# Layer 0's cross-attention: PSUM in four pairs of banks, and one instruction for two heads' banks

## The chip, the cores and the metric

The kernel runs on one NeuronCore of a Trainium2 chip. Its engines work side by side, each on its own queue of instructions: TensorE (PE; its weight loads are shown apart as PEld) multiplies matrices, VectorE (DVE) and ScalarE (ACT) work on elements, GpSimd (POOL) does the same and issues some of the DMAs, SyncE (SP) issues the others. TensorE writes its results to PSUM, a small memory that VectorE and ScalarE read. This kernel uses it as eight banks of 512 float32 columns by 128 partitions. An engine that needs the result, or the buffer, of another waits for a semaphore. The metric is device time in microseconds (us), the median of several runs.

## The reference

The reference is a two-layer decoder on 32 sequences of 100 tokens of width 256. Each layer has self-attention, cross-attention to a context, and a mixture of experts, all in float32. The change lies in the cross-attention of Layer 0, with 16 heads of 16 channels and a context of 361 positions of width 128:

```python
Q = (x @ Wq.T).reshape(B, xN, NUM_HEADS, HEAD_DIM)
KV = (z @ Wkv.T).reshape(B, zN, 2, NUM_HEADS, HEAD_DIM)
K = KV[:, :, 0]
V = KV[:, :, 1]
attn = jnp.einsum('bqhd,bkhd->bhqk', Q, K) * SCALE
attn = jax.nn.softmax(attn, axis=-1)
O = jnp.einsum('bhqk,bkhd->bqhd', attn, V).reshape(B, xN, DIM)
return O @ Wo.T
```

For each sequence and head this is a table of 100 queries by 361 positions, of which each row's maximum, exponentials and sum are taken.

## The kernel before

The function `l0_xattn` does this part. All eight banks of PSUM are one ring of single banks (`banks("l0x", t=8)`). Every producer on TensorE asks for a bank by `bank(...)`, and when the ring is empty its first weight load waits until the last reader of the bank that is handed out is done. Banks come back in the order in which their readers are planned to finish.

The main loop runs over 64 items M, two per sequence b: M = 2b + c, where c picks eight of the 16 heads. Those eight heads are done in two groups j of four. The four heads of a group lie in four blocks of 32 rows (`rows_of(r)`), so that their matmuls run side by side on TensorE. A head has 16 channels. The other 16 rows of its block carry a row of ones and the negated maximum, so that the second product below comes out with the maximum already subtracted.

The order of TensorE's queue is written out by hand (`manual_schedule`); that of the other engines is set by the framework's planner. For item M, TensorE gets:

- `maxima(M - 1)`: two transposes of the maxima (L543), which VectorE adds to the queries (L545). One bank.
- `scores(M, 0)`: queries by keys for four heads, into four banks. VectorE takes each bank's maximum over 361 positions, 100x1 from 100x361 (L535): one instruction for each head.
- `turned(M - 1, 0)`: the same product turned, positions by queries, in three pieces of 121 positions by 100 queries for each of the four heads, into four banks. ScalarE takes the exponential of each bank, 121x300 (L557): one instruction for each head. GpSimd adds up pieces for the sums (L561, L562).
- `values(M - 2)`: exponentials by values (L571) and by ones (L578), into one bank, which ScalarE copies (L583).
- `scores(M, 1)` and `turned(M - 1, 1)`: the other four heads, four banks each.
- the extras: `keys` for the next sequence (one bank; ScalarE makes two masked copies, L507), then either `out` (the output projection of a finished tile of 128 tokens, when c is 0; VectorE adds it to x, L261) or `queries` (when c is 1, in every other pair of items; ScalarE, L500), or neither, then `vals` for the next sequence (one bank; two or four copies by ScalarE, L520).
- at some items a piece of the next part's work: the turning of normed rows (L231), or the routing's logits (L1414).

So an item asks for 21 banks or a few more, out of eight. `keys` runs in 62 of the items, `out` or `queries` right behind it in 36. The helper `mm` (L156) issues the matmuls of most of these. In the profile `ps_t<-k,qT` at L156 is `scores`, `ps_t<-q,k` is `turned`, `ps_t<-cT,wB` is `keys`, `ps_t<-wB,zT` is `out`, `ps_t<-xnT,wB` is `queries` and `ps_t<-wB,cT` is `vals`. One matmul in the code shows up there as two.

The reciprocal of the sums (L588, in `divided`) is made to stand behind the last reduction of a group with j = 0, by an explicit dependency.

Of the kernel before, what the change touches and what calls it, by code (L numbers as in the profile page):

```python
# [9 lines left out]
F32 = mybir.dt.float32  # L10
I32 = mybir.dt.int32
U32 = mybir.dt.uint32
AF = mybir.ActivationFunctionType
ALU = mybir.AluOpType
AX = mybir.AxisListType

P = 128
NB = 32
T = 100
NT = NB * T  # L20
NF = NT // P
D = 256
NK = D // P
H = 16
L = 361
NKC = 3
KC0, KC = 121, 124
# [72 lines left out]
class Kernel:  # L100
# [26 lines left out]
        return self.tc.tile_pool(name=f"ps{name}", bufs=1, space=bass.MemoryType.PSUM)  # L127

    def bank(self, tag):
        if tag not in self.n_banks:  # L130
            tag = "t"
        return self.psum.tile([P, 512], F32, tag=tag, name=f"ps_{tag}", bufs=self.n_banks[tag])

    def bank_s(self):
        return self.bank("s")
# [91 lines left out]
    def norm_turn(self, f, n, xn, bank):  # L227
        pt = bank[:, : NK * n * P].rearrange("p (k c) -> p k c", k=NK)
        for k in range(NK):
            for j in range(n):  # L230
                self.nc.tensor.transpose(  # L231
                    pt[:, k, j * P : (j + 1) * P], xn[:, j, k * P : (k + 1) * P], self.ident,
                )
        self.evac(self.xnT[:, :, f * P : (f + n) * P], pt)
# [197 lines left out]
    def l0_xattn(self):  # L432
        nc, tc, a = self.nc, self.tc, self.a
        with ExitStack() as st:
            self.psum = st.enter_context(self.banks("l0x", t=8))
            w = self.wts.tile([P, 3584], F32, tag="wB", name="wB0")
            wq = w[:, :512].rearrange("p (k n) -> p k n", k=NK)
            wk, wv = w[:, 512:768], w[:, 768:1024]
# [40 lines left out]
            ks = [cp.tile([P, 2, 2, LP0], F32, tag=f"k{i}", name=f"k{i}") for i in range(3)]  # L479
            ms = [cp.tile([T, 2, P], F32, tag=f"m{i}", name=f"m{i}") for i in range(3)]  # L480
# [2 lines left out]
            for t in ks:  # L483
                nc.gpsimd.memset(t[:, :, :, L:], 0.0)
            later = deque()
            ctx, q, q2, e, es = {}, {}, {}, {}, {}
            self.z_begin(pool, 2)

            def load(b):
# [10 lines left out]
                    nc.scalar.activation(t[:, c, j, :], pm, AF.Copy, scale=quarter[:, j : j + 1])  # L500

            def keys(b, c):
                pm = self.bank_t()[:, :L]
                self.mm(pm, [(wk[:, c * P : (c + 1) * P], ctx[b][:, :L])])
                t = ks[b % 3]
                for j in range(2):
                    nc.scalar.activation(  # L507
                        t[:, c, j, :L], pm, AF.Identity, bias=one[:, j : j + 1], scale=own[:, j : j + 1]
                    )

            def vals(b, c0, n):
                pm = self.bank_t()[:KC0, : n * D].rearrange("p (c d) -> p c d", c=n)
                for i in range(n):
                    c = c0 + i
                    self.mm(pm[:, i, :], [(ctx[b][:, c * KC0 : (c + 1) * KC0], wv)])
                pv = pm.rearrange("p c (h j d) -> p c h j d", j=2, d=16)
                v = vs[b % 3][:, c0 : c0 + n].rearrange("p c (h j) e -> p c h j e", j=2)
                for j in range(2):
                    for i in range(n):
                        nc.scalar.copy(v[:, i, :, j, 16 * j : 16 * j + 16], pv[:, i, :, j, :])  # L520

            def rows_of(r):
                return slice(32 * r, 32 * r + 32)


            def scores(M, j):
                b, c = divmod(M, 2)
                cols = slice((b % 4) * T, (b % 4 + 1) * T)
                ps = [self.bank("r")[:T, :L] for _ in range(4)]
                for r in range(4):  # L530
                    self.mm(ps[r], [(q[b // 4][rows_of(r), c, j, cols], ks[b % 3][rows_of(r), c, j, :L])])
                m = ms[M % 3]
                for r in range(4):
                    o = 32 * r + 16 * (1 - j)
                    got = nc.vector.tensor_reduce(m[:, j, o : o + 1], ps[r], AX.X, ALU.max, negate=True)  # L535
                return got

            def maxima(M):
# [7 lines left out]

            def turned(M, j):
                b, c = divmod(M, 2)
                ps = [self.bank("r")[:KC0, : NKC * T] for _ in range(4)]
                for i in range(NKC):  # L550
                    for r in range(4):
                        self.mm(ps[r][:, i * T : (i + 1) * T], [(
                            ks[b % 3][rows_of(r), c, j, i * KC0 : (i + 1) * KC0], q2[M][rows_of(r), j, :]
                        )])
                t = e[M, j] = pool.tile([KC0, 4, NKC, T], F32, tag="e", name="e", bufs=5)
                for r in range(4):
                    nc.scalar.activation(t[:, r], ps[r].rearrange("p (c t) -> p c t", c=NKC), AF.Exp)  # L557

                n = L - 2 * KC0
                s = es[M, j] = pool.tile([KC0, 4, T], F32, tag="es", name="es", bufs=4)  # L560
                nc.gpsimd.tensor_tensor(s, t[:, :, 0, :], t[:, :, 1, :], ALU.add)  # L561
                nc.gpsimd.tensor_tensor(s[:n], s[:n], t[:n, :, 2, :], ALU.add)  # L562
# [48 lines left out]
            def extras(b):  # L611

                k0, k1, v0, v1, o, x = [None] * 6
                if b + 1 < NB:
                    k0, k1 = (lambda: keys(b + 1, 0)), (lambda: keys(b + 1, 1))
                    v0, v1 = (lambda: vals(b + 1, 0, 2)), (lambda: vals(b + 1, 2, 1))
                if b > 1 and tile_of(b - 2) is not None:
                    o = lambda: out(tile_of(b - 2))
                b0, i = b // 4 * 4, b % 4
                if i < 2 and b0 + 4 < NB:  # L620
                    x = lambda: queries(b0 + 4, i)
                return k0, v0, o, k1, v1, x
# [11 lines left out]
            with tc.manual_schedule(engines={mybir.EngineType.PE}):  # L634
# [4 lines left out]
                for c in range(2):  # L639
                    keys(0, c)  # L640
                vals(0, 0, 2)
                vals(0, 2, 1)
                last = 2 * NB
                for M in range(last + 2):
                    b, c = divmod(M, 2)
                    if c == 0:
                        if b + 2 < NB:
                            load(b + 2)
                        ex = extras(b)
                    if 0 < M <= last:  # L650
                        maxima(M - 1)
                    if M in norms:
                        f, *at = norms[M]
                        f(*at)
                    for j in range(2):

                        got = scores(M, j) if M < last else None
                        if j == 0 and M > 2:
                            divided(M - 3, zs, got)
                        if 0 < M <= last:  # L660
                            turned(M - 1, j)
                        if j == 0 and M > 1:
                            zs = values(M - 2)
                    if M == last + 1:
                        divided(M - 2, zs, None)
                    for i in (0, 2, 1):
                        if ex[3 * c + i]:
                            ex[3 * c + i]()
                    if M not in norms or len(later) > 3:
                        for _ in range(1 + (len(later) > 3)):  # L670
                            if later:
                                later.popleft()()
# [1422 lines left out]
```

## Time and profile before

| | |
|---|---|
| median of three runs | 2956.52 us (2954.38 to 2960.02) |
| the profiled execution | 2956.08 us, its span 2954.3 us |
| granted TensorE clock, mean | 0.984 |
| PE busy over the span | 97% |
| VectorE, ScalarE, GpSimd busy | 61%, 48%, 31% |
| the changed stage | 585 to 1065 us of the span |
| L535, reductions of a bank | 512 of 524 ns, 239.6 us busy |
| L557, exponentials of a bank | 512 of 426 ns, 173.9 us busy |

A row of groups gives line, engine, operation, what is written from what, shapes, the number of instructions, their busy time together and the mean length of one, and the idle time just before them with who ended it. A timeline merges instructions of a kind that follow each other: start, length from the first's start to the last's end, engine, line, operation, count. Instructions of one engine overlap: the four reductions of a group take 1.85 us together, less than four times one.

### The profile page before, as it was taken

How to read it: one execution, taken by the hardware profiler on the slowest of the kernel's cores; microseconds unless marked ns; L12 is line 12 of the kernel's file. 1: busy time of each engine (PE TensorE's matmuls, PEld its weight loads, DVE VectorE, ACT ScalarE, POOL GpSimd, SP SyncE). 2: the span in 40 equal slices, each digit the busy share in tenths (PEclk: the TensorE clock that was granted, in tenths of full speed). 3: DMA queues.
4: the chain of work that ended last, by engine and by line, in shares of the span. 5: the costliest groups of instructions: out<-in, count | busy, mean ns of one | idle time of the engine just before them, and what ended most of it. 6: DMA issues, size and time to landing. Idle time of an engine off the chain costs nothing. (4 is left out here: it accounts for less than half of the span.)

```text
span 2954.3 us, 66469 instructions
## 1 busy us (share of the span) xinstructions
PE 2851.3 (97%) x26012; PEld 2172.6 (74%) x26012; DVE 1787.6 (61%) x5120; ACT 1412.4 (48%) x4261; POOL 913.0 (31%) x1040
## 2 busy tenths in 40 slices
PE   8999999999999999999998999999999999999993
PEld 7777777677777766888886667777777777776672
DVE  6666665577777762222224878676676776776553
ACT  5555555467676641222223224565666565657320
POOL 3222221266666536100003621011302213123373
PEclk9999999999999989999999999999999999999996
DMA  9880000000000004564553100010000000000396
GB/s 319 269 290 1 1 1 1 12 15 16 16 16 16 10 29 147 191 223 181 194 215 112 49 4 10 6 38 25 26 10 13 10 9 16 12 11 5 97 227 189
DMA packets 127510, 224.11 MB, mean 76 GB/s; under 512 B 39470, under 2 KB 105446, under 8 KB 120401
## 3 DMA queue, kind: packets, MB, share of 16 engines
q1 hardware_dynamic: 97264, 125.64, 13.3%
q0 software_dynamic: 26640, 90.80, 9.3%
q8 instruction: 210, 3.44, 0.5%
q10 hardware_dynamic: 3280, 3.28, 0.3%
q14 instruction: 116, 0.94, 0.1%
HBM read 152.09 MB, written 112.56 MB: 90 GB/s over the span
## 5 line engine op out<-in xcount | busy, mean ns | idle before, releaser
L1691 POOL DMA_INDIRECT x_d<-xr,slot x200 | 195.4, 977 | 676.0 <-ACT eT L786 556.3
L156 PE MATMUL ps_t<-xnT,wA 128*128 128x200 f32 (+1 forms) x1608 | 330.9, 350 | 1.5 <-DMA wA<-in_wq 1.0
L156 PE MATMUL ps_t<-cT,q 128*128 128x361 f32 x832 | 317.3, 470 | 0.0
L786 ACT COPY eT<-ps_t 124x384 f32<-124x384 f32 (+1 forms) x416 | 193.6, 474 | 224.7 <-PE ps_t L785 224.5
L156 PEld LDWEIGHTS ps_t<-xnT,wA 128*128 128x128 f32 x1608 | 272.1, 191 | 32.4 <-issue 14.5
L776 ACT ACTIVATE wBx<-ps_t,m 128x361 f32<-128x361 f32 x416 | 235.8, 568 | 121.7 <-DVE m L773 117.7
L535 DVE TENSOR_REDUCE m<-ps_t 100x1 f32<-100x361 f32 x512 | 239.6, 524 | 48.3 <-PE ps_t L156 48.1
L156 PE MATMUL ps_t<-xT,w 128*128 128x256 f32 (+1 forms) x1276 | 260.2, 364 | 0.7 <-ACT xT L150 0.7
L773 DVE TENSOR_REDUCE m<-ps_t 128x1 f32<-128x361 f32 x416 | 218.3, 526 | 60.3 <-PE ps_t L156 58.3
L156 PEld LDWEIGHTS ps_t<-xT,w 128*128 128x128 f32 x1276 | 223.7, 190 | 36.2 <-issue 9.3
L785 PEld LDWEIGHTS ps_t<-ident,wBx 128*124 128x124 f32 x1248 | 156.1, 139 | 123.4 <-issue 68.2
L358 POOL TENSOR_TENSOR e<-e,rz 100x400 f32<-100x400 f32 x128 | 109.3, 854 | 406.3 <-DVE rz L357 396.8
L557 ACT ACTIVATE e<-ps_t 121x300 f32<-121x300 f32 x512 | 173.9, 426 | 119.0 <-PE ps_t L156 118.9
L785 PE MATMUL ps_t<-ident,wBx 128*124 128x128 f32 x1248 | 203.9, 275 | 5.3 <-DVE m L1627 2.1
L354 ACT ACTIVATE e<-s,m 100x100 f32<-100x100 f32 x512 | 186.1, 365 | 20.7 <-DVE m L348 20.0
L156 PE MATMUL ps_t<-wA,cT 128*124 128x512 f32 x384 | 195.5, 597 | 0.0
L778 DVE TENSOR_SCALAR wBx<-wBx,sums 128x361 f32<-128x361 f32 x416 | 172.9, 416 | 9.9
L1344 DVE TENSOR_TENSOR h<-ps_t,g 128x256 f32<-128x256 f32 (+1 forms) x145 | 58.2, 401 | 188.4 <-ACT g L1343 188.4
L156 PEld LDWEIGHTS ps_t<-q,k 32*121 32x121 f32 x3072 | 127.9, 181 | 36.0 <-issue 11.3
L797 PEld LDWEIGHTS ps_t<-eT,v 124*64 124x64 f32 x3072 | 133.1, 137 | 16.4 <-ACT wBx L776 5.6
L1343 ACT ACTIVATE g<-ps_t 128x256 f32<-128x256 f32 (+1 forms) x145 | 52.9, 365 | 190.9 <-PE ps_t L156 190.9
L1280 POOL DMA_INDIRECT w<-w_d,wid x29 | 29.5, 1017 | 371.0 <-PE ps_t L1371 337.4
(329 smaller groups left out, 5817.8 us busy)
## 6 DMA issues: line engine op xcount, KB each, us to landing
x_d<-fill SPq DMA_DIRECT2D x16, 1284.0 KB, 22.2
we<-in_wexp SPq DMA_DIRECT2D x32, 384.0 KB, 4.6
cT<-in_ctxT SPq DMA_DIRECT2D x64, 186.0 KB, 2.3
xe_d<-zero SPq DMA_DIRECT2D x8, 1024.0 KB, 16.3
xe<-x_d SPq DMA_DIRECT2D x24, 321.0 KB, 3.8
sum<-fill SPq DMA_DIRECT2D x10, 640.0 KB, 8.9
xe<-xe_d SPq DMA_DIRECT2D x24, 256.0 KB, 2.7
y_d<-y SPq DMA_DIRECT2D x24, 256.0 KB, 8.4
```

Source lines behind the costliest of these rows:

```text
L156: self.nc.tensor.matmul(out, lhsT=l, rhs=r, start=(i == 0), stop=(i == n - 1))
L354: nc.scalar.activation(t[:, i, :], s[:, i, :], AF.Exp, bias=m[:, i : i + 1], accum_out=rz[:, i : i + 1])
L358: nc.gpsimd.tensor_tensor(t[:, h, :], t[:, h, :], self.last(rz[:, h], T), ALU.mult)
L535: got = nc.vector.tensor_reduce(m[:, j, o : o + 1], ps[r], AX.X, ALU.max, negate=True)
L557: nc.scalar.activation(t[:, r], ps[r].rearrange("p (c t) -> p c t", c=NKC), AF.Exp)
L773: self.after = nc.vector.tensor_reduce(m, ps, AX.X, ALU.max, negate=True)
L776: nc.scalar.activation(t, ps, AF.Exp, bias=m, accum_out=z)
L778: nc.vector.tensor_scalar(t, t, z, None, ALU.mult)
L785: nc.tensor.transpose(pt[:, c, :], es[n % 5][:, c * KC : (c + 1) * KC], self.ident)
L786: self.after = nc.scalar.copy(eT[:, :, i * P : i * P + w], pt[:, :, :w])
L797: nc.tensor.matmul(pz[64 * j : 64 * j + 64, i, :], lhsT=v[:, c, h * 64 : (h + 1) * 64], rhs=eT[:, c, o : o + T], start=(c == 0), stop=(c = ...
L1691: got = nc.gpsimd.indirect_dma_start(out=self.x1_d[:, :], out_offset=bass.IndirectOffsetOnAxis(ap=slot[:, j, k : k + 1], axis=0), in_=xr[: ...
```

## The change

PSUM is given out in this stage as four pairs of neighbouring banks in place of eight single ones. A caller of `bank` gets the first bank of a pair of its own; the second then lies unused. `scores` and `turned` take two pairs each, with two heads in a pair, and each pair is read by one instruction: one maximum over both heads' banks (100x2 from 100x722), one exponential over both (121x600). `keys` takes a pair and leaves its second bank to the `vals` that follow it, so that the two share a pair.

```diff
     def bank(self, tag):
+        if not self.n_banks:
+            return self.pair()[:, 0, :]
...
+    def pair(self):
+        return self.psum.tile([P, 2, 512], F32, tag="t", name="ps_t", bufs=4)
...
-            self.psum = st.enter_context(self.banks("l0x", t=8))
+            self.psum = st.enter_context(self.banks("l0x"))
...
             def keys(b, c):
-                pm = self.bank_t()[:, :L]
+                both[c] = self.pair()
+                pm = both[c][:, 0, :L]
...
             def vals(b, c0, n):
-                pm = self.bank_t()[:KC0, : n * D].rearrange("p (c d) -> p c d", c=n)
+                pm = both[c0 // 2][:KC0, 1, : n * D].rearrange("p (c d) -> p c d", c=n)
...
-                ps = [self.bank("r")[:T, :L] for _ in range(4)]
+                ps = [self.pair()[:T, :, :L] for _ in range(2)]
                 for r in range(4):
-                    self.mm(ps[r], [(q[b // 4][rows_of(r), c, j, cols], ks[b % 3][rows_of(r), c, j, :L])])
-                m = ms[M % 3]
-                for r in range(4):
-                    o = 32 * r + 16 * (1 - j)
-                    got = nc.vector.tensor_reduce(m[:, j, o : o + 1], ps[r], AX.X, ALU.max, negate=True)
+                    self.mm(
+                        ps[r // 2][:, r % 2, :],
+                        [(q[b // 4][rows_of(r), c, j, cols], ks[b % 3][rows_of(r), c, j, :L])],
+                    )
+                m = ms[M % 3].rearrange("t j (h r e) -> t j h r e", h=2, r=2)
+                for h in range(2):
+                    got = nc.vector.tensor_reduce(
+                        m[:, j, h, :, 16 * (1 - j)], ps[h], AX.X, ALU.max, negate=True
+                    )
...
-                ps = [self.bank("r")[:KC0, : NKC * T] for _ in range(4)]
+                ps = [self.pair()[:KC0, :, : NKC * T] for _ in range(2)]
                 for i in range(NKC):
                     for r in range(4):
-                        self.mm(ps[r][:, i * T : (i + 1) * T], [(
+                        self.mm(ps[r // 2][:, r % 2, i * T : (i + 1) * T], [(
...
-                for r in range(4):
-                    nc.scalar.activation(t[:, r], ps[r].rearrange("p (c t) -> p c t", c=NKC), AF.Exp)
+                for h in range(2):
+                    two = t[:, 2 * h : 2 * h + 2].rearrange("p r c t -> p r (c t)")
+                    nc.scalar.activation(two, ps[h], AF.Exp)
```

More of the change, by code (lines that the diff above doesn't have):

```diff
@@ L485, in l0_xattn @@
             later = deque()
-            ctx, q, q2, e, es = {}, {}, {}, {}, {}
+            ctx, q, q2, e, es, both = {}, {}, {}, {}, {}, {}
             self.z_begin(pool, 2)
```

## The prediction

> **What bounds the kernel now.** I read the page's 40 slices first, then the busy table of this stage, then the timeline of two of its steps, then its waits, and last the rows that price the instructions. The change touches only Layer 0's cross-attention, which runs from 585 to 1065 us. The slices say that TensorE is full nearly all the time; VectorE and ScalarE are not.
>
> ```profile
> PE   8999999999999999999998999999999999999993
> DVE  6666665577777762222224878676676776776553
> ACT  5555555467676641222223224565666565657320
> ```
>
> In the stage alone, the columns being the stretch, its length, and the busy time of PE, weight loads, VectorE, ScalarE and GpSimd:
>
> ```profile
> 600.00:1060.00 460.00, 449.93 (x8533) 350.60 (x8523) 349.49 (x851) 310.81 (x898) 278.68 (x351) 1.00 0.05 14
> ```
>
> PE is busy for 98% of it at a granted clock of 1.00, VectorE for 76%, ScalarE for 68%. So the stage's length is that of PE's queue plus PE's waits, and work taken from VectorE or ScalarE is worth nothing by itself. What such an instruction does to the time is settled by when it gives its bank back to PE. The timeline (start, length, engine, line, what, how many; in brackets the idle time before and who ended it) shows that:
>
> ```profile
> 715.61 0.87 PE L156 MATMUL ps_t<-k,qT 32*100 32x361 f32 x8
> 716.49 1.85 DVE L535 TENSOR_REDUCE m<-ps_t 100x1 f32<-100x361 f32 x4 [0.63 <-PE ps_t L156]
> 717.08 0.30 PEld L156 LDWEIGHTS ps_t<-cT,wB 128*128 128x128 f32 x2 [0.16 <-DVE m L535]
> 717.08 0.88 PE L156 MATMUL ps_t<-cT,wB 128*128 128x361 f32 x2
> 717.11 1.36 ACT L557 ACTIVATE e<-ps_t 121x300 f32<-121x300 f32 x4 [0.99 <-PE ps_t L156]
> 717.52 0.89 PEld L156 LDWEIGHTS ps_t<-wB,zT 128*128 128x128 f32 x4
> 717.79 1.03 PE L156 MATMUL ps_t<-wB,zT 128*128 128x256 f32 x4
> 718.32 1.22 ACT L507 ACTIVATE k<-ps_t,one,own 128x361 f32<-128x361 f32 x2
> ...
> 720.67 1.42 DVE L535 TENSOR_REDUCE m<-ps_t 100x1 f32<-100x361 f32 x3
> 721.35 1.02 PEld L571 LDWEIGHTS ps_t<-e,v 121*32 121x32 f32 x48
> ```
>
> The four scores of a group end together (715.61 + 0.87 = 716.48), and VectorE reduces their banks one after another. The first reduction ends at 717.02; 0.05 later PE starts `keys` (cT,wB), in that very bank. `keys` already waits for the first bank to come back: eight banks are just enough. The waits of the stage agree (total us, times, longest):
>
> ```profile
> PEld ps_t L156 <- DVE m L535: 8.6, 51, 0.5
> PEld ps_t L571 <- DVE m L535: 8.0, 14, 1.4
> PE ps_t L571 <- DVE m L535: 5.6, 7, 1.2
> ```
>
> 51 of the 62 calls of `keys` (L156) wait for a maximum, and so do about 20 calls of `values` (L571).
>
> **The change, part by part.** *Fewer, longer reductions.* 512 become 256, each over two banks. Their length:
>
> ```profile
> L535 DVE TENSOR_REDUCE m<-ps_t 100x1 f32<-100x361 f32 x512 | 239.6, 524 | 48.3 <-PE ps_t L156 48.1
> L348 DVE TENSOR_REDUCE m<-s 100x8 f32<-100x800 f32 x64 | 63.0, 985 | 2.0
> L557 ACT ACTIVATE e<-ps_t 121x300 f32<-121x300 f32 x512 | 173.9, 426 | 119.0 <-PE ps_t L156 118.9
> ```
>
> 361 columns take 524 ns and 800 take 985, so a column costs 461/439 = 1.05 ns and 722 columns 524 + 361 x 1.05 = 903 ns. Bounds: 524 (the second bank free) and 967 (two of today's in a row, 524 + 443, since four take 1.85 us and so follow each other by 0.443). I take 903, by the 800-column row. A whole group then takes 0.903 + 0.82 = 1.72 us, not 1.85: 0.13 saved per group, 128 x 0.13 = 17 us of VectorE. Nothing on PE waits for the end of a group, so this is worth 0; it would count only if VectorE were the bound. *Exponentials:* the four take 1.36 us, one 0.426, so they already follow each other by 0.311. Two of 600 columns take 1.22 to 1.36 by the same reasoning. Worth 0: PE takes the first of those banks again 1.5 us after they begin (715.61 against 714.07 in the step shown).
>
> [...]
>
> *`keys` waits for two banks.* With four pairs, `keys` is the first taker after two pairs of scores and two of `turned`, and must wait for one of those. The earliest is the first score pair, 0.903 us after the reduction starts in place of 0.533: +0.36 where it waits today. I went through all 62 calls and took, for each, start of the first reduction + 0.90 + 0.05 less the start of its weight load, where positive: 56 are delayed, 20.3 us in all. Behind it in PE's queue stand `out` or `queries`, `vals`, the turning of the maxima and the next scores, so all of PE is late by it; ScalarE's copies of the keys, which wait for PE, begin later too. At 0.967 instead of 0.903 it is 24; at 0.524 it is 0.
>
> *`values` waits the same way.* At 720.67 the reductions start, at 721.35 `values` start; the pair is back at 720.67 + 0.95 = 721.62: +0.27. The same count over 64 calls: 35 late, 11.2 us.
>
> *`out` and `queries`.* One of them follows `keys` in 36 steps and takes the second score pair, back at 1.72 + 0.05 = 1.77 us after the reductions' start. `keys`, started at 0.95, frees PE after 0.71 (0.41 + 0.30 for its two passes) at 1.66; and a weight load that has waited is not hidden (+0.105, as the first pass of `keys` today: 0.41 against 0.30). 1.77 + 0.105 - 1.66 = 0.215, x 36 = 7.7 us. If the pair of the first exponentials is taken instead (back at 1.35), 0.
>
> *`vals` in the second bank of `keys`' pair.* It takes no new pair and waits for nothing new, provided that one bank's reader does not hold up the other bank's writer. But the pair comes back only after the last copy of the values (720.49 in the step shown, against the next scores at 719.78). The second half of the next `turned` is what takes it, at about 720.54 against 720.37; +0.17, which `values` wait for anyway: 0. If instead the second half of the scores took it, `values` would come 0.54 late in place of 0.27, at up to 27 steps: +7 to +15.
>
> *Table loads.* After the stage's 6 norm roots ScalarE reloads its table (1283 ns) and the exponentials come late; the next scores then wait for a pair, not a bank, one spacing of 0.31 longer: 6 x 0.3 = 1.8 us.
>
> Sum: 20.3 + 11.2 + 7.7 + 0 + 1.8 = 41 us. The profiled execution took 2956.08 (span 2954.3 and 1.8 around it), 0.4 below the median of 2956.52. 2956.1 + 41 = 2997.
>
> **The rivals.** *Absorbed (2976).* Only `keys` is late, and what follows finds its pair free in the time lost. For it: after a late `keys` the next waits start later too. Against: a reduction starts when PE ends the scores, so every gate moves along with PE. 20 us.
>
> *The value copies gate the scores (3012).* As above, 0.54 x 27 = 15 on top of 2997, if none of it falls together with `values`' own wait. For it: 0.77 us of copies (L520) end after the next scores begin. Against: `out` and `queries` give their pairs back sooner, and the planner hands out what is free first.
>
> *A pair is guarded as a whole (3045).* If `vals`' matmul had to wait until ScalarE has read the keys: 718.32 + 1.22 = 719.54 and 0.05, where without it PE would come to `vals` 0.58 later than today's 718.44, at 719.02. 0.57 there, and up to 1.1 where no `out` or `queries` stands between them; 0.77 as a middle, x 62 = 48 on top of 2997. No row of before has two banks in one tile, so it can't be excluded.
>
> *Faster (2941).* VectorE is the real clock: PE's waits for L535 in this stage are 8.6 + 8.0 + 5.6 = 22 us, mostly in steps where rows of a norm push the reductions back; if groups that end 0.13 earlier pull these in, up to 15 us go. It decides only where a two-bank reduction takes less than 0.53 us, so that the first pair returns as soon as the first bank does now; the 800-column row says 0.90.
>
> **How the numbers follow.** A measurement of this kernel tells about 0.2% (6 us) from no change. As summed (2985 to 3008): 0.50. Absorbed (2965 to 2985): 0.17. Value copies (3008 to 3030): 0.14. Pair as a whole (3030 to 3065): 0.09. Faster: 0.06. Same, by shares of all of these: 0.04. The range takes the first three, 2966 to 3030, and leaves out 0.2: the last three and a sliver of the second. Faster 0.06, same 0.04, slower 0.90.
>
> **What would show it.** The new profile should have 256 reductions of about 903 ns with a group of 1.72 us; PE's weight loads of `keys` should start 0.05 us after a *two-bank* reduction's end, with idle time near 0.5 us before them, where it is 0.16 now; `values` should wait in over 50 steps; the two score groups of one step should lie as far apart as now, but for that. VectorE and ScalarE should be busy for less time in a longer stage. I am wrong if the reductions take much under 0.9, if `vals` waits for L507, or if the stage (480 us now) grows by less than 25 or more than 60 us.

## The result and the profile after

The changed kernel takes 3051.84 us (3050.38 to 3052.94) against 2955.45 before: a ratio of 1.0326, interval 1.0314 to 1.0338, or 96 us slower. The forecast was 2997 (2966 to 3030): the direction was right, the size less than half. Measured again (after_again below), the two stood at 3053.91 and 2958.22, 1.0327 (1.0311 to 1.0343).

All of it is in the changed stage. From the first reduction's start to the last one's end it took 477.8 us before and takes 573.0 now, 95.2 more. The slices of the page after, eight in a row (the stage) at 0.8 where all were at 0.9:

```profile
PE   8999999888888889999999899999999999999993
DVE  6666656466556555222222687776766666776553
ACT  5555545455555543122212323565655666666320
```

The stage alone, before and after (stretch, length, busy time of PE, weight loads, VectorE, ScalarE and GpSimd, granted clock, DMA share and GB/s):

```profile
585.00:1065.00 480.00, 468.97 (x8748) 363.74 (x8744) 362.53 (x883) 325.16 (x938) 287.03 (x362) 0.99 0.05 14
585.00:1165.00 580.00, 497.65 (x8865) 362.23 (x8864) 348.66 (x639) 321.69 (x689) 289.91 (x364) 0.96 0.04 12
```

VectorE has 14 us less to do than in the stage before (17 was the prediction's figure) and ScalarE some 3 us less (the longer window holds a little other work); PE stands idle for 82 of the 580 us, where it was 11 of 480. What it waits for, in total us, times, longest; two rows of before, then three of after:

```profile
PE ps_t L156 <- DVE m L535: 0.9, 3, 0.4
PE ps_t L156 <- ACT k L507: 0.2, 1, 0.2
PE ps_t L161 <- ACT k L513: 38.6, 48, 1.6
PE ps_t L161 <- DVE m L543: 23.0, 60, 0.7
PE ps_t L582 <- DVE m L543: 18.4, 42, 1.2
```

L513 is ScalarE's copies of the keys (L507 before), and the one that waits is `vals`. The next line is nearly all `keys`, the last `values`; both are waits for a maximum. The timeline of one step after the change:

```profile
726.75 1.73 DVE L543 TENSOR_REDUCE m<-ps_t 100x2 f32<-100x722 f32 x2 [0.77 <-PE ps_t L161]
727.71 0.30 PEld L161 LDWEIGHTS ps_t<-cT,wB 128*128 128x128 f32 x2 [0.55 <-DVE m L543]
728.53 0.73 PEld L161 LDWEIGHTS ps_t<-wB,zT 128*128 128x128 f32 x4 [0.52 <-DVE m L543]
728.53 1.13 PE L161 MATMUL ps_t<-wB,zT 128*128 128x256 f32 x4
728.62 1.20 ACT L513 ACTIVATE k<-ps_t,one,own 128x361 f32<-128x361 f32 x2
729.87 1.12 PE L161 MATMUL ps_t<-wB,cT 128*121 128x256 f32 x4 [0.21 <-ACT k L513]
```

`keys` (cT,wB) start 0.96 us after the reductions do, 0.59 before. `out` (wB,zT) waits for the second pair of maxima: its matmuls come 0.82 us after those of `keys`, 0.71 before, and, their weights not loaded ahead, take 1.13, 1.03 before. And `vals` (wB,cT) starts at 729.87, 0.05 after the keys' copies end at 728.62 + 1.20 = 729.82. It writes the other bank of the pair that they read. Where no `out` or `queries` lies between, PE stands still for 1.29 us in place of the 0.21 here:

```profile
719.29 0.87 PE L161 MATMUL ps_t<-cT,wB 128*128 128x361 f32 x2 [0.39 <-DVE m L543]
720.21 1.20 ACT L513 ACTIVATE k<-ps_t,one,own 128x361 f32<-128x361 f32 x2
721.45 0.69 PE L161 MATMUL ps_t<-wB,cT 128*121 128x256 f32 x2 [1.29 <-ACT k L513]
```

The joined instructions came out as priced: a reduction takes 905 ns (priced at 903), and two exponentials together 1.23 us in the steps read (priced at 1.22 to 1.36):

```profile
L543 DVE TENSOR_REDUCE m<-ps_t 100x2 f32<-100x722 f32 x256 | 221.8, 905 | 78.2 <-PE ps_t L161 78.0
L568 ACT ACTIVATE e<-ps_t 121x600 f32<-121x600 f32 x256 | 157.7, 668 | 141.3 <-PE ps_t L161 141.3
```

### The profile page after: what moved, and what is told of

Read it like the earlier page. It is cut to its first block, busy times and chain, and to the rows that moved or that the text cites. A ratio compares the mean times of both kernels' runs of the same rounds, so it can differ in the third digit from the quotient of the medians.

```text
span 3051.2 us, 65927 instructions
## 1 busy us (share of the span) xinstructions
PE 2870.7 (94%) x26012; PEld 2163.6 (71%) x26012; DVE 1770.2 (58%) x4864; ACT 1408.5 (46%) x4005; POOL 914.4 (30%) x1040
## 5 line engine op out<-in xcount | busy, mean ns | idle before, releaser
L543 DVE TENSOR_REDUCE m<-ps_t 100x2 f32<-100x722 f32 x256 | 221.8, 905 | 78.2 <-PE ps_t L161 78.0
L784 DVE TENSOR_REDUCE m<-ps_t 128x1 f32<-128x361 f32 x416 | 218.3, 526 | 59.7 <-PE ps_t L161 57.8
L568 ACT ACTIVATE e<-ps_t 121x600 f32<-121x600 f32 x256 | 157.7, 668 | 141.3 <-PE ps_t L161 141.3
L161 PEld LDWEIGHTS ps_t<-q,k 32*121 32x121 f32 x3072 | 121.9, 185 | 28.3 <-DVE q L555 11.2
```

What stands on the lines that cost most here:

```text
L161: self.nc.tensor.matmul(out, lhsT=l, rhs=r, start=(i == 0), stop=(i == n - 1))
L543: got = nc.vector.tensor_reduce(m[:, j, h, :, 16 * (1 - j)], ps[h], AX.X, ALU.max, negate=True)
L568: nc.scalar.activation(two, ps[h], AF.Exp)
L784: self.after = nc.vector.tensor_reduce(m, ps, AX.X, ALU.max, negate=True)
```

## The experiments

Chips differ: the kernel before took 2987.62 us on the one that ran vals_free, vals_own_pair and the two kv kernels, and 2956.01 and 2958.22 on the two others. So times are compared as ratios to the kernel before on the same chip, and beside them as lengths of the stage (first reduction's start to last one's end in the profile).

### vals_free: the wait of vals taken away

```diff
 # keys: the two copies
+    tc.add_to_no_dep_group(f"keys{b}_{c}", got.ins)
 # vals: each matmul
+    tc.declare_no_dep(got.ins, group=f"keys{b}_{c0 // 2}", reason="the pair's other bank")
```

The framework then sets no wait between those copies and `vals`; all other waits stay.

> The changed kernel, except that the matmul of vals is told not to wait for the copies of the keys, which read the pair's other bank. Theory A (a pair is guarded as a whole, and that wait is the larger half of the loss): PE's idle time before vals for L513, 37 us after the change, goes, and with it some of the half-clock stretches in the stage: 2990 to 3015 us, near the forecast's 2997. Theory B (the ring of four pairs is short in itself; a wait taken away in one place comes back at the next taker): 3035 to 3052 us.

Measured: 3023.06 us against 2987.62, 1.0120 of before (1.0096 to 1.0144). Run again beside the changed kernel on one chip:

> The changed kernel once more, to stand beside vals_free on one chip: 1.031 to 1.034 of before.

> vals_free once more, beside the changed kernel and before. Theory A in its sizes (the guard of the whole pair costs 37 us of waiting and some 18 us of half clock; the later return of the pairs costs the other 40): 1.012 to 1.015 of before, 50 to 60 us under the changed kernel.

Measured: 3053.91 us (1.0327) and 2996.90 us (1.0129, 1.0114 to 1.0145). The stage takes 517.5 us, not 573.8. What PE waits for in vals_free_again:

```profile
PE ps_t L161 <- DVE m L547: 22.9, 60, 0.7
PE ps_t L586 <- DVE m L547: 18.0, 31, 1.2
```

The line of the keys' copies is gone, and the two waits for maxima stay as they were, 23 and 18 us. So nothing came back at the next taker, as theory B would have had it. 57 of the 96 us go with that one wait. The two banks have nothing to do with each other in the program; the wait comes only from the framework, which ordered accesses to this tile of two banks as if it were one.

### vals_own_pair: no sharing

```diff
-                pm = both[c0 // 2][:KC0, 1, : n * D].rearrange("p (c d) -> p c d", c=n)
+                pm = self.pair()[:KC0, 0, : n * D].rearrange("p (c d) -> p c d", c=n)
```

> The changed kernel, with a pair of its own for vals, so that the pair of the keys is not shared and its other bank lies unused. Theory A: the wait for the keys' copies goes, a wait for the third pair in order comes, which is back about 0.4 us before it is wanted: 2995 to 3020 us. Theory B: one more pair per item out of four, so slower than the changed kernel: 3055 to 3080 us.

Measured: 3029.45 us, 1.0147 (1.0124 to 1.0169), a stage of 520.3 us, 2.8 more than vals_free's. One more pair per item costs next to nothing. Where `vals` follow `keys` directly they start 0.81 us after them in the mean of 26 steps, 0.74 in vals_free_again; behind `out` or `queries` they lose nothing. Which pair they get, the trace does not show. Theory B is out: the ring is not short in that sense. Sharing a pair, meant to spare one, was the dear part.

### kv_pair_t6 and kv_single_t6: the same two banks as one tile and as two

Both start from the kernel before, with single instructions, and in both the first sequence's `vals` stand right behind each of its `keys`.

```diff
 # kv_pair_t6 (six single banks besides)
+                both[c] = self.psum.tile([P, 2, 512], F32, tag="kv", name="ps_kv", bufs=1)
+                pm = both[c][:, 0, :L]
...
+                pm = both[c0 // 2][:KC0, 1, : n * D].rearrange("p (c d) -> p c d", c=n)
 # kv_single_t6 (six single banks besides)
+                pm = self.bank("k")[:, :L]
...
+                pm = self.bank("v")[:KC0, : n * D].rearrange("p (c d) -> p c d", c=n)
```

> The kernel before, all instructions as they were, but with keys and vals in the two banks of one tile of their own and six single banks for the rest. To be compared with kv_single_t6, which uses the same banks as two tiles. Theory A: slower than kv_single_t6 by 62 waits of 0.5 to 0.9 us, 30 to 55 us. Theory B: the same within 6 us. Both are slower than before, since six banks do not hold two groups of four: 3010 to 3090 us.

> The kernel before with one single bank for keys, one for vals, and six for the rest. Theory A and B alike: slower than before, because the last two heads of turned must wait for reductions (0.5 to 1 us in each of 128 groups, less 8 us since keys no longer wait): 3000 to 3060 us.

Measured: 3244.84 us (1.0884, 1.0836 to 1.0932) and 3124.71 us (1.0457, 1.0430 to 1.0483), 120 us apart; stages of 727.0 and 623.4 us in the profiled executions. The sign is theory A's; the size, 104 us in the stage, is twice what it allowed. The waits of kv_pair_t6 hold only half of it; in kv_single_t6 the first line does not appear and the second reads 53.3:

```profile
PE ps_kv L156 <- ACT k L508: 57.8, 62, 1.5
PE ps_t L156 <- DVE m L536: 51.1, 120, 1.0
```

The other half is in PE's own speed. The two stages, kv_pair_t6 and then kv_single_t6:

```profile
590.00:1320.00 730.00, 620.17 (x8737) 450.87 (x8738) 358.92 (x878) 326.11 (x929) 287.71 (x360) 0.90 0.04 9
```

```profile
588.00:1212.00 624.00, 566.65 (x8732) 425.82 (x8728) 359.89 (x878) 323.63 (x930) 287.87 (x360) 0.96 0.04 11
```

The same matmuls take 54 us longer, at a mean granted clock of 0.90 in place of 0.96. By the trace's clock records PE ran at half its clock for 144.9 us of the one stage and 47.8 of the other; 97 us more at half the clock hold up to 48.5 us less work, an estimate from these two figures. 57.8 + 48.5 = 106 at most, against 103.6 measured. That the waits bring the half clock is not shown by this pair; the next run tests it.

### keep_busy: PE given something to do in the wait

The changed kernel, its wait of `vals` left as it is.

```diff
+                    tc.add_to_no_dep_group(f"keys{b}_{c}", got.ins)     # keys: the two copies
...
+                for _ in range(fill):            # vals: ahead of its own matmuls
+                    got = nc.tensor.matmul(
+                        pm[:, 0, :], lhsT=ctx[b][:, :KC0], rhs=wv, start=True, stop=True
+                    )
+                    tc.declare_no_dep(got.ins, group=f"keys{b}_{c0 // 2}", reason="the pair's other bank")
 # fill is 2 where no out or queries stands between keys and vals, else 0
```

> The changed kernel, and where vals follows keys directly, two extra matmuls (128x121 by 128x256) into the bank of vals are issued ahead of it; their result is overwritten. They do not wait for the keys' copies; vals still does. They fill about 0.86 us of a wait of 1.3 us in some 26 steps. If the half-clock stretches of the stage (41 us at half the clock, against 4 before) come from these waits and cost about 18 us, most of them go: 5 to 18 us faster than the changed kernel, 1.026 to 1.031 of before. If they come from elsewhere or cost nothing: the same as the changed kernel or slower, 1.032 to 1.040.

Measured: 1.0276 (1.0260 to 1.0292), 15 us less than the changed kernel by ratio. The stage takes 560.4 us in place of 573.0, with more matmuls in it. A step of keep_busy:

```profile
717.91 0.88 PE L161 MATMUL ps_t<-cT,wB 128*128 128x361 f32 x2 [0.38 <-DVE m L549]
718.62 1.03 PE L521 MATMUL ps_t<-wB,cT 128*121 128x256 f32 x4
718.83 1.19 ACT L513 ACTIVATE k<-ps_t,one,own 128x361 f32<-128x361 f32 x2
720.07 0.69 PE L161 MATMUL ps_t<-wB,cT 128*121 128x256 f32 x2 [0.42 <-ACT k L513]
```

The extra matmuls (L521) fill part of the wait, and `vals` still start right after the copies: 2.16 us after `keys`, here (720.07 less 717.91) as in the changed kernel (721.45 less 719.29). So the step itself gains nothing. PE's clock stands at half for 6.8 us of this stage, against 41.0 in the changed kernel's and 4.4 before; in vals_free_again, with the wait taken away, it is 6.8 too. So here the long waits bring half-clock stretches with them, and those cost something of their own: 34 us at half the clock (41.0 less 6.8) are up to 17 us by estimate. The measured 12.6 us in the stage are the gain less whatever the extra matmuls cost.

In the changed kernel's stage the half clock comes in ten stretches at 0.5, eight of 3.4 us and two of 6.8. A matmul of the scores takes 870 ns in the mean inside them (48 matmuls) and 501 outside. No wait of PE there is longer than 1.6 us, and several lie in a step: 0.19, 0.39 and 1.29 us in the 7 us ahead of the first stretch, which begins at 606.4.

### short_max: a pair given back as early as a bank was

From vals_free; the maximum is taken over the first 180 of the 361 positions only, so that part of the computation is left out.

```diff
-                        m[:, j, h, :, 16 * (1 - j)], ps[h], AX.X, ALU.max, negate=True
+                        m[:, j, h, :, 16 * (1 - j)], ps[h][:, :, : L // 2], AX.X, ALU.max, negate=True
```

> vals_free with each reduction over the first 180 of the 361 positions of both banks (360 columns, so about 524 ns as one bank's took before). Left out: the other positions' part in the maximum. Theory A (the rest of the loss, 35 to 40 us, is that a pair comes back 0.37 us later than a bank did, at keys, out, queries and values): nearly all of it goes, 0.995 to 1.005 of before. Theory B (the rest is the ring of four pairs itself, or the longer exponentials): it stays, 1.008 to 1.014.

Measured: 1.0008 (0.9999 to 1.0017), a stage of 478.9 us against 477.8 before. With two-bank reductions of 528 ns the longest waits left are

```profile
PE ps_t L586 <- DVE m L547: 7.7, 14, 0.9
PE ps_t L161 <- ACT v L530: 3.8, 12, 1.4
```

Pairs, joined exponentials and the shared pair are all still there. So the rest of the loss, 39 us, goes with the length of the reductions, and at the places named: from the start of `keys` to the end of `out` a step takes 1.74 us in the mean, as before, and 1.95 in vals_free_again. One thing is not parted: a shorter reduction also ends its group earlier and leaves VectorE less to do (253 us in the stage, 363 before), and that could cover a loss of a few us elsewhere.

### two_reads: pairs without joined instructions

From vals_free.

```diff
+                for r in range(4):
+                    o = 32 * r + 16 * (1 - j)
+                    got = nc.vector.tensor_reduce(
+                        m[:, j, o : o + 1], ps[r // 2][:, r % 2, :], AX.X, ALU.max, negate=True
+                    )
...
+                for r in range(4):
+                    nc.scalar.activation(
+                        t[:, r], ps[r // 2][:, r % 2, :].rearrange("p (c t) -> p c t", c=NKC), AF.Exp
+                    )
```

> vals_free with the pairs kept, but each bank read by an instruction of its own again, 512 reductions and 512 exponentials. Theory A: a pair then comes back at 0.967 us in place of 0.903 after its reductions begin, so 0.06 us later at some 110 waits: 3 to 10 us over vals_free, 1.012 to 1.017 of before. Theory C (joining the instructions saves time by itself, and the pairs spoil it): 17 us or more over vals_free, 1.018 or more.

Measured: 1.0165 (1.0149 to 1.0180); the stage takes 527.7 us, 10.2 over vals_free's. The waits go from 22.9 and 18.0 to

```profile
PE ps_t L161 <- DVE m L548: 25.9, 58, 0.8
PE ps_t L588 <- DVE m L548: 20.8, 31, 1.6
```

That is the upper end of theory A and below theory C's 17. So once banks are held in pairs, joining the reads is the better way, since it gives the pair back sooner: by 0.06 us over the 89 waits of these two lines, 5.3 us, and by 5.8 they grew. Of the other 4 us, 3 lie in PE's busy time; they are not explained here. Single banks with single reads, as before, are still 48 us better.

### keys_s1 and keys_s0: can the kernel before lose its waits?

Both keep the eight single banks and move `keys` in PE's order, since `keys` was what waited for the first maximum.

```diff
                     for j in range(2):
                         got = scores(M, j) if M < last else None
+                        if j == 1 and ex[3 * c]:      # keys_s0: j == 0
+                            ex[3 * c]()
...
-                    for i in (0, 2, 1):
+                    for i in (2, 1):
```

> The kernel before with its single banks, and keys moved from behind turned(M-1,1) to between scores(M,1) and turned(M-1,1), where the bank that it takes has long been read. Theory A (PE's waits for the first bank are what the stage pays): the 51 waits of 0.15 us for a maximum before keys go, 4 to 9 us, 0.997 to 0.9985 of before. Against it: ScalarE now makes the keys' copies (1.22 us) ahead of the exponentials, so that the scores of the next item wait for them where no out or queries stands between: up to 26 x 0.8 = 20 us slower, 1.002 to 1.007.

> The kernel before with its single banks, and keys moved between scores(M,0) and turned(M-1,0), where turned has to wait for the queries with the maxima added. If that wait is free time on PE and keys fill it: 5 to 15 us faster than before, 0.995 to 0.998. If a matmul over all 128 rows between two groups that run in blocks of 32 rows costs what it did in keys_s1 (0.3 us per item, where PE's busy time and not its idle time grew): 1.003 to 1.008. The next taker of a bank after turned(M-1,1) then waits in place of keys, so its 0.15 us stay.

Measured: 1.0067 (1.0054 to 1.0081) and 1.0041 (1.0028 to 1.0055): both slower than before, by 20 and 12 us. In keys_s1 PE's idle time stays near 12 us (11 before) while its busy time grows. Its stage, to be held against 468.97 of 480 before:

```profile
585.00:1085.00 500.00, 487.79 (x8740) 345.67 (x8737) 366.56 (x878) 325.77 (x938) 287.48 (x361) 0.99 0.05 14
```

```profile
722.87 0.30 PEld L156 LDWEIGHTS ps_t<-cT,wB 128*128 128x128 f32 x2 [0.53 <-ACT zs L583]
723.67 0.72 PEld L156 LDWEIGHTS ps_t<-q,k 32*121 32x121 f32 x24 [0.51 <-issue]
```

Before, `turned` (q,k) loaded its weights 0.38 us after the scores began (715.99 against 715.61 in the step read before) and beside them, in blocks of 32 rows; here its load stands 0.51 us for no wait on another engine, behind `keys` that fill all rows. The load of `keys` stands still too, 0.53 us; the copy that the row names (L583) had ended at 722.58, 0.29 us earlier, so that its bank is hardly the reason. That the change between the two kinds of matmul is why is argued from these lines, not shown apart, and for keys_s0 not looked into. The wait of about 0.17 us (8.6 us in 51) that the move was to save was the smaller price. No version here beats the kernel before.

## Why the prediction was wrong, and where it was right

*The step that failed* is "`vals` in the second bank of `keys`' pair", costed at nothing "provided that one bank's reader does not hold up the other bank's writer". It did, since the framework guarded the pair as a whole; vals_free_again, with just that wait removed, puts it at 57 us. It was the rival "a pair is guarded as a whole", given 0.09 and 3045 us (48 us on top). That the rival's time came so near is in part chance: it priced 62 waits of 0.77 us and no clock, and the runs show 48 waits of 0.8 us, 38.6 in all, weight loads no longer hidden, and a PE at half clock, which the forecast had nowhere. Two of its own signs of being wrong came true: `vals` wait for the keys' copies, and the stage grew by more than 60 us.

*`keys`: right.* Priced at 20.3; the idle time of PE ahead of their matmuls, for a maximum, grew from 0.4 to 21.3 in vals_free_again, 20.9. *`out` and `queries`: right.* Priced at 0.215 each, 7.7 in all; the step shown has 0.82 + 1.13 against 0.71 + 1.03, 0.21. Over all steps of vals_free_again it is 0.21 in the 22 with `out` and 0.15 in the 14 with `queries`, 6.7, which lies in PE's busy time. *`values`: right.* Priced at 11.2; 5.6 grew to 18.0, 12.4. *Table loads: not seen.* Priced at 1.8; PE's weight loads waited 3.3 us for the exponentials before and 3.6 in vals_free.

*Reductions and exponentials: right.* 903 ns priced, 905 measured; a group 1.72, measured 1.73. That all this is worth 0 on the path is right in so far as no gain shows; two_reads adds that, inside pairs, the earlier end is worth 6 to 10 us, which the sum held as 903 in place of 967.

*The sum of the other terms: right.* 41 us was the forecast for everything but the guard. vals_free_again is the changed kernel without the guard: 38.7 us over before (2996.90 less 2958.22), 39.7 in the stage. The second half of the loss was thus a mechanism left at 0.09, not a mis-sized term.

*The value copies* did not gate the scores: in vals_free_again PE waits 1.9 us for them, twice. *Absorbed* is refuted by the same run, *faster* by all. The 22 us of *faster* were also counted too high: the seven waits of L571's matmuls (5.6) are the same as seven of the fourteen of its weight loads (8.0), and so 14 calls of `values` waited, not about 20.

The balance of the stage, 95.2 us, goes by vals_free_again and keep_busy. 39.7 are for pairs that come back later (short_max takes that to 1.1). keep_busy, which keeps the guard and has as little half clock as vals_free_again, stands 42.9 above that run (560.4 less 517.5): that is the guard's wait, 38.6 of PE standing idle after the change, and some 6 of weight loads that are no longer hidden. For `vals` right behind `keys` take 0.69 us in the step shown, and in vals_free_again

```profile
706.07 0.59 PE L522 MATMUL ps_t<-wB,cT 128*121 128x256 f32 x2
```

0.1 less, as 1.12 against 1.03 behind `out`, in 62 steps. The last 12.6 (573.0 less 560.4) are the half clock's, less whatever the extra matmuls cost.

## What to carry to other kernels

Before two operands are put into one tile to save buffers, find out by what unit the framework orders accesses: here two banks in one tile made a matmul wait for a reader of the other bank, at the price of 57 us, the half clock among them. An instruction that reads two buffers at once gave both back late here, after 905 ns where one buffer took 524; VectorE (busy for 349 of the 580 us) and ScalarE (322) were not the bound, so the 14 us of VectorE and 3 of ScalarE that were saved were worth nothing, and TensorE, which was, paid for the later return: 39.7 us of the stage. And a wait on TensorE was here not only its length: look at the granted clock of the stage too, 0.96 after the change and 0.99 before.

## What the runs showed of the hardware

The granted TensorE clock fell to half in stretches of 3.4 and 6.8 us inside a stage where PE was never idle for more than 1.6 us at a time, 86% busy in all: 41.0 us of half clock after the change, 4.4 before, 6.8 with the new wait taken away (vals_free_again), 144.9 in kv_pair_t6 (0.90 mean clock). Filling part of the waits with matmuls whose result is thrown away brought it to 6.8 us and the kernel down by 15 us.
